# A graph layer's edge loop: its entry, its row buffers and the loop for wide groups rearranged

## The chip, the cores and the metric

The kernel runs on one core of a Trainium2 chip, in one launch. The metric is the device time of that launch in microseconds (us), as a median over runs. The engines are TensorE (PE, with its weight loads as PEld), VectorE (DVE), ScalarE (ACT), GpSimd (POOL) and SyncE (SP, which only issues transfers here).

## The reference

One graph layer with a residual and a layer norm. `x` has 6250 nodes of 128 values, `src` and `dst` are the ends of 100000 edges, sorted by `dst`.

```python
msg_in = concatenate([x[src], x[dst]], -1)                    # [100000, 256]
h = relu(msg_in @ Wm1 + bm1)                                  # hidden 256
h = relu(h @ Wm2 + bm2)                                       # 256
messages = h @ Wm3 + bm3                                      # 128
agg = segment_sum(messages, dst) / clip(count(dst), 1)        # mean over a node's edges
upd = relu(concatenate([x, agg], -1) @ Wn1 + bn1) @ Wn2 + bn2
out = layernorm(x + (x + upd))
```

All data are float32.

## The kernel before

**Algebra.** The first product is taken per node and not per edge: table A is `x @ Wm1[:128]` (float32, in DRAM, `atab`) and table B is `x @ Wm1[128:]` (split into bf16 terms, in DRAM, `btab`). An edge's hidden row is A's row of its source plus B's row of its destination. The third product is linear, so the second hidden layer is summed per destination first, in `acc`, and multiplied with `Wm3` per node afterwards.

**Stage 1 (0 to about 74 us).** Thirteen blocks of 512 nodes: load x, turn it (`turn`), A table (`a_table`), B table (`b_table`, `b_terms`), stores of both (`b_stores`, on SP's queue), and preparation of the edges' indices on DVE. `weights(i)` loads four weights. `x_part(b, ...)` is the x half of the update's first layer for one block: two matmuls of 128x512 (L355) into two PSUM banks, and an eviction each, on ACT (L358) or DVE (L360). Twelve of the blocks are done at places listed by hand: ten in `X_BEHIND` behind the table matmuls, block 9 (`X_FIRST`) in the edge loop's first step and block 10 (`X_END`, the generator `rest`) in its last. `pb3` is a small product of a weight and a bias (L451), added to `b3` as `b23`. `destinations(g, ...)` fetches the `dst` values of two groups, broadcast over the partitions, into `db` (256 KB, two transfers of 128 KB on ACT's queue). Three of these are fetched in the last three blocks of stage 1, into the three buffers of `db`.

**Stage 2, the edge loop (about 75 to 1072 us).** The edges form 196 groups of 512, handled in 98 pairs. It is a Python loop, so the program is straight-line; the order of instructions on PE and DVE is the order in which they are written (manual schedules), and the loop is a pipeline by hand over i, with p = i - 1:

- `fetch` of pair i: `rows` (2 buffers) holds for each group four gathered rows of A and the loaded rows of B side by side. Eight indirect gathers on POOL (L492) and eight loads from `btab` (L498) on SP's queue; for pair 0 the second group's four loads are on ACT's queue, behind the wait for B's stores like the other four.
- `hot`: one-hot matrices from `db` on DVE (L516, L519), one pair ahead.
- `first_layer` of pair p: 32 transposes of gathered A rows into PSUM (`ph`, L533; one buffer, so the previous pair's evictions must be done), 16 bf16 matmuls that add B's rows through the one-hots (L540), and four evictions with relu into `h1` on ACT (L546).
- For p = 0, X_FIRST's `x_part` follows (one eviction on ACT, one on DVE).
- `part_of(summed(p - 2))`: the sum over edges of a destination window (L565), copied on ACT (L573).
- `second_layer` of pair p - 1: L555 on PE, L557 (bias and relu by a maximum) on DVE, into `h2s`.
- `turned(p - 3)` and `add_up`: transposes (L584) and DVE's additions into `acc` at places read from registers (L594). `load_bases` fills those registers.
- `clear(n)`: DVE memsets of parts of `acc` (L638), before `first_layer` of pair 0 and at the end of steps 1 and 2.
- In the last step (p - 2 = 97) the two halves of X_END stand before and behind L565.

**Wide groups.** Where a group's destinations span more nodes than one window takes, a dynamic loop (L702, `tc.For_i(0, groups)`) adds the further windows. `groups` is 0 for these inputs, so its body is not run, but each engine passes the loop's entry and exit.

**Stage 3, the nodes (about 1073 to 1144 us).** Per block: `products` (L773: `Wm3` on `acc`; L775 on DVE; POOL's L778 multiplies with the reciprocal of the counts), `hidden` (L787, L788), `second` (L813, L815), and the norm (`moments`, `scaled`, store). The first two blocks take their reciprocals on DVE from `acc` (L767, L768). For the others the counts go from `acc` to `rcol` (SP, L754), reciprocals of those are stored to `rtab` (L760), and `rc` is loaded from there, broadcast (L770).

Of the kernel before, what the change touches and what calls it, by code (L numbers as in the profile page):

```python
# [19 lines left out]
P = 128  # L20
# [7 lines left out]
def kernel(  # L28
# [121 lines left out]
    with tc.tile_pool(name="prep", bufs=1) as prep, tc.tile_pool(  # L150
# [34 lines left out]
            nc.gpsimd.dma_start(bu1, bn1.rearrange("(c p) -> p c", p=P))  # L185

        def weights(block):
            for t in (wu1, w3, w2):
                nc.vector.tensor_copy(t[:, 0, :1], xT[:, block * 4 * P:block * 4 * P + 1])
            nc.gpsimd.dma_start(nb2[:, 0, :], bm2.rearrange("(o h) -> o h", o=1).to_broadcast([P, H]))  # L190
            nc.sync.dma_start(wu1, wn1.rearrange("(k p) h -> p k h", p=P))
            nc.sync.dma_start(w3, wm3.rearrange("(k p) h -> p k h", p=P))
            nc.sync.dma_start(w2, wm2.rearrange("(k p) h -> p k h", p=P))

        nc.vector.memset(xT[:, N:], 0.0)

# [178 lines left out]
        def destinations(g, ng, dst_row):  # L375

            db = ld.tile([P, 2, 2 * P], I32, name="db", bufs=3)
            if isinstance(g, int) and g < 6:

                nc.vector.tensor_copy(db[:, 0, :1], srcT[:, 0, :1])  # L380
            for h in range(2):
                edges = dst_row[:, ds(g * GE, ng * GE)].rearrange("o (s e) -> o s e", s=ng)
                edges = edges[:, :, h * 2 * P:(h + 1) * 2 * P]
                nc.scalar.dma_start(db[h * NQ:(h + 1) * NQ, :ng, :], edges.to_broadcast([NQ, ng, 2 * P]))
            return [db[:, k, :] for k in range(ng)]
# [20 lines left out]
        for i in range(BLOCKS):  # L406
            if i in X_LOADS:
                load_x(*X_LOADS[i], behind=i)
                if X_LOADS[i][1] == BLOCKS - 1:
                    nc.sync.dma_start(x_sb[:N - NTF * P, NTF, :], x[NTF * P:, :])  # L410
            for n, t0 in enumerate(range(4 * i, min(4 * i + 4, NT), 2)):

                if n == (i == 0) and i + 1 < BLOCKS:
                    turn(4 * i + 4)
                a_table(t0)
            b_stores()
            for _ in range(min(len(blank), 3 if i < BEHIND else 1)):
                nc.gpsimd.memset(blank.pop(0), 0.0)
            if i == BEHIND + 1:
                weights(i)  # L420
            if i == INDICES:
                starts()
            if i - INDICES in (1, 2):
                columns(i - INDICES - 1)
                partition_bases(i - INDICES - 1)
            if i == BLOCKS - 1:
                nc.scalar.copy(tilei, base[0:1].rearrange("p r w -> p (r w)"))
                nc.gpsimd.tensor_scalar(nb2, nb2, -1.0, None, op0=ALU.mult)
            if i >= BEHIND:
                b_block(i - BEHIND)  # L430
            if BLOCKS - 3 <= i:
                early.append(destinations(2 * len(early), 2, dst_row))
        assert not blank
        behind = list(X_BEHIND)
        with tc.manual_schedule(engines={ENG.DVE}):
            for n, j in enumerate(range(BLOCKS - BEHIND, BLOCKS)):
                if n < 4:
                    whole(x_part(behind.pop(0), bank_pb, (nc.scalar, (nc.scalar, nc.vector)[n % 2])))
                b_block(j)
                b_stores()  # L440
            b_terms()
            b_stores()
        stores.close()


        turns.enter_context(tc.manual_schedule(engines={ENG.DVE}))
        for n, b in enumerate(behind):
            whole(x_part(b, bank_pb, (nc.vector if n >= len(behind) - 2 else nc.scalar, nc.vector)))
        pb3 = pp.tile([P, 1], F32, name="pb3", tag="pp")
        for c in range(HC):  # L450
            nc.tensor.matmul(pb3, w3[:, c, :], b2[:, c:c + 1], start=(c == 0), stop=(c == HC - 1))  # L451
        nc.vector.tensor_add(b23, b3, pb3)

# [10 lines left out]
    with edge, tc.tile_pool(name="wk", bufs=2) as wk, tc.tile_pool(  # L464
# [19 lines left out]
        def fetch(groups, queues):  # L484


            rows = ld.tile([P, 2, (GT + 1) * H], F32, name="rows", bufs=2)
            got = []
            for i, ((idx, firsts), queue) in enumerate(zip(groups, queues)):
                ag = rows[:, i, :GT * H].rearrange("p (j h) -> p j h", j=GT)  # L490
# [4 lines left out]
                bw = rows[:, i, GT * H:].bitcast(BF16).rearrange("p (k h) -> p k h", k=2)  # L495
                for j, first in enumerate(firsts):
                    terms = btab[ds(first, WB + 1)].rearrange("n c h -> (n c) h")
                    queue.dma_start(bw[j // 2 * NQ:(j // 2 + 1) * NQ, j % 2, :], terms[:NQ])  # L498
# [25 lines left out]

        halves = [slice(h * NQ, (h + 1) * NQ) for h in range(2)]

        def first_layer(got, ohts, nts):
            ph = p1.tile([P, 2, 2, HC, 2 * P], F32, name="ph")
            for i, ((ag, bw), nt) in enumerate(zip(got, nts)):
                for c in range(HC):  # L530
                    for u in range(GT):
                        for h in range(nt // 2):
                            nc.tensor.matmul(ph[:, i, h, c, u * NQ:(u + 1) * NQ], ag[halves[h], u, c * P:(c + 1) * P],  # L533
                                             ident[halves[h], halves[h]], is_transpose=True,
                                             start=(c == 0 and u == 0), stop=False, skip_group_check=True)
            for i, ((ag, bw), nt) in enumerate(zip(got, nts)):
                for c in range(HC):
                    for k in range(2):
# [4 lines left out]
            for i in reversed(range(len(nts))):  # L543
                nh = nts[i] // 2
                for c in range(HC):
                    nc.scalar.activation(h1[:, i, c, :nh * 2 * P].rearrange("p (h e) -> p h e", h=nh),  # L546
                                         ph[:, i, :nh, c, :], AF.Relu, bias=b1[:, c:c + 1])
            return h1

        def second_layer(h1, h2, nt):  # L550
# [81 lines left out]
        def summed(p):  # L632
            s = st[p]
            return sums([(s["ohs"][i], h2s[i], s["nts"][i]) for i in range(2)])

        slots = list(range(SLOTS))

        def clear(n):  # L638
# [5 lines left out]
        for i in range(NP + 4):  # L644
# [54 lines left out]


        dpad_row = dpad.rearrange("(o e) -> o e", o=1)
        with tc.For_i(0, groups, 1) as g:  # L702
            more = nc.values_load(
                morei[0:1, ds(g, 1)], min_val=0, max_val=N // 16,
                skip_runtime_bounds_check_because="the difference of two nodes over 16")
            with tc.For_i(0, more, 1):
                for t, by in ((tilei[0:1, ds(g * GT, GT)], float(WB)), (pbase[:, ds(g, 1), :], float(WB)),
                              (dloc[:, ds(g, 1), :], -float(WB))):
                    nc.vector.tensor_scalar(t, t, by, None, op0=ALU.add)
                idx = wk.tile([P, GT], I32, name="idx")  # L710
                nc.vector.tensor_copy(idx, srcT[:, ds(g, 1), :].rearrange("p o j -> p (o j)"))
                pbc = wk.tile([P, 2], F32, name="pbc")
                nc.vector.tensor_copy(pbc, pbase[:, ds(g, 1), :].rearrange("p o k -> p (o k)"))
                dl = wk.tile([P, GT], F32, name="dl")
                nc.vector.tensor_copy(dl, dloc[:, ds(g, 1), :].rearrange("p o j -> p (o j)"))

                ti = wk.tile([1, GT], I32, name="ti")
                nc.vector.tensor_scalar_min(ti, tilei[0:1, ds(g * GT, GT)], float(N - 1))
                got = fetch([(idx, load_bases(ti, GT, ENG.SP))], [nc.sync])
                db, = destinations(g, 1, dpad_row)  # L720
                ohts, (oh,) = hot([(db, pbc, dl, GT)])
                h1 = first_layer(got, ohts, [GT])
                second_layer(h1[:, 0], h2s[0], GT)
                part = part_of(sums([(oh, h2s[0], GT)]), [GT])
                add_up(turned(part, [GT]), [load_bases(ti, GT, ENG.DVE)], [GT])


    NB = 4 * P
# [226 lines left out]
```

## Time and profile before

| | |
|---|---|
| Median of 6 runs | 1149.25 us (1147.84 to 1155.75) |
| The profiled execution | 1150.46 us |
| Its span, first to last instruction | 1148.4 us |
| Mean granted clock of TensorE in it | 0.995 |
| ACT, DVE and POOL busy in it | 378.6, 683.0 and 810.6 us |
| Start of the first L533 of pairs 0 to 5 | 75.33, 83.23, 92.08, 103.12, 113.84, 123.9 us |
| One pair from then on | 10.06 us |
| POOL's eight gathers of a pair | start every 10.05 us |
| B's last store: issued, landed | 67.85, 72.49 us |
| Pair 0: last L540 ends, its four L546 | 80.0, 80.16 to 82.58 us |
| First L773 of the node stage | 1073.39 us |

All rows below the median are of one profiled execution. A pair's start is the start of its first L533 matmul. The granted clock is the share of full speed that TensorE was given in a stretch. In an answer on waits, "A <- B: sum, times, longest" says that operations of A waited for B; a "q" behind an engine's name is its sequencer or queue. In a timeline each line has a start, the time from there to the end of the last of its instructions, the engine, the line of code and the operation, the number of instructions, and in brackets an idle time ahead of it and what ended it.

### The profile page before, as it was taken

Reading aid. Unit: us, or ns where it says so; the run is one execution under the profiler, and the core shown is the slowest. Engines: PE = TensorE matmul, PEld = TensorE weight load, DVE = VectorE, ACT = ScalarE, POOL = GpSimd, SP = SyncE. Lnnn points to the kernel's source line nnn. Section 1 sums busy time; section 2 is a strip of 40 time slices with the busy share of each in tenths; the row PEclk is TensorE's granted clock in tenths of the full one; section 3 lists DMA queues with packets and bytes.
Section 4 is the critical chain, followed back from the end, with each engine's and each line's share of the span. In section 5 each row is a group of like instructions: output and inputs, shape, how many; then the busy total and the mean of one; then the engine's idle time right before and its main releaser. Section 6 shows DMA issues by size and latency. Waiting matters only on the chain. (4 is left out here: it accounts for less than half of the span.)

```text
span 1148.4 us, 32176 instructions
## 1 busy us (share of the span) xinstructions
PE 1133.0 (99%) x11222; PEld 913.9 (80%) x11223; DVE 683.0 (59%) x2073; ACT 378.6 (33%) x768; POOL 810.6 (71%) x871
## 2 busy tenths in 40 slices
PE   9989999999999999999999999999999999999997
PEld 8757888888888888888888888888888888888566
DVE  5775556655555565555555555555555555555687
ACT  6752333322233332223333223333322333322165
POOL 8867777777777777777777777777777777773222
PEclk9999999999999999999999999999999999999899
DMA  8966666566666656666665656556555555552343
GB/s 283 366 227 183 170 174 172 157 177 178 169 171 176 175 153 178 178 170 170 176 166 155 168 162 161 162 154 156 158 158 161 162 160 155 155 157 63 102 126 103
DMA packets 167752, 193.67 MB, mean 169 GB/s; under 512 B 31074, under 2 KB 133428, under 8 KB 167572
## 3 DMA queue, kind: packets, MB, share of 16 engines
q0 software_dynamic: 38160, 103.75, 33.7%
q1 hardware_dynamic: 100640, 61.84, 18.4%
q10 hardware_dynamic: 28788, 26.01, 7.7%
q8 instruction: 89, 1.46, 0.5%
q14 instruction: 75, 0.61, 0.2%
HBM read 168.97 MB, written 22.88 MB: 167 GB/s over the span
## 5 line engine op out<-in xcount | busy, mean ns | idle before, releaser
L492 POOL DMA_INDIRECT rows<-atab,srcT x784 | 747.4, 953 | 244.7 <-issue 185.2
L555 PE MATMUL bank<-w,h 128*128 128x256 f32 x3128 | 701.3, 382 | 0.7 <-DVE acc L594 0.6
L555 PEld LDWEIGHTS bank<-w,h 128*128 128x128 f32 x3128 | 586.5, 190 | 116.5 <-PE bank L565 40.3
L557 DVE TENSOR_TENSOR h<-bank,nb 128x512 f32<-128x512 f32 x391 | 270.9, 693 | 349.6 <-PE bank L555 329.8
L546 ACT ACTIVATE h<-ph,b 128x512 f32<-128x512 f32 x392 | 236.7, 686 | 694.0 <-PE ph L540 665.6
L594 DVE TENSOR_TENSOR acc<-acc,bank 128x63 f32 x782 | 172.7, 221 | 69.1 <-DVE h L557 34.9
L533 PE MATMUL ph<-ident,rows 64*128 64x64 f32 x3128 | 114.2, 223 | 1.3 <-DMA rows<-atab,srcT 0.7
L533 PEld LDWEIGHTS ph<-ident,rows 64*128 64x128 f32 x3128 | 105.5, 139 | 2.9 <-ACT x_sb L358 1.0
L565 PE MATMUL bank<-h,oh 128*32 128x257 f32 x1564 | 105.5, 386 | 0.2 <-ACT x_sb L358 0.2
L516 DVE TENSOR_SCALAR oht<-db,pbase 128x128 bf16<-128x128 int32 x392 | 95.2, 294 | 0.4
L584 PEld LDWEIGHTS bank<-ident,part 64*128 64x128 f32 x1173 | 43.1, 136 | 32.9 <-issue 32.2
L573 ACT COPY part<-bank 128x257 f32<-128x257 f32 x196 | 65.3, 401 | 7.1 <-PE bank L565 7.1
L778 POOL TENSOR_TENSOR agg<-total,rc 128x512 f32<-128x512 f32 (+2 forms) x15 | 16.0, 1070 | 72.2 <-DVE total L775 37.3
L565 PEld LDWEIGHTS bank<-h,oh 128*32 128x32 f32 x1564 | 40.8, 109 | 28.3 <-DVE acc L594 0.8
L540 PE MATMUL ph<-oht,rows 64*128 64x128 bf16 x1564 | 60.9, 217 | 2.4 <-DMA rows<-btab 2.4
L584 PE MATMUL bank<-ident,part 64*128 64x64 f32 x1173 | 56.5, 229 | 0.0
L519 DVE TENSOR_TENSOR oh<-iota_n,dloc 128x128 f32<-128x128 f32 x196 | 55.5, 283 | 0.0
L540 PEld LDWEIGHTS <-rows 64*128 64x128 bf16 x1564 | 49.0, 95 | 2.8 <-DMA rows<-btab 2.7
L258 PE MATMUL pbt<-w,xT 128*128 128x256 f32 x196 | 46.0, 381 | 0.9 <-DVE rest L285 0.6
L258 PEld LDWEIGHTS pbt<-w,xT 128*128 128x128 f32 x196 | 36.0, 190 | 7.4 <-DVE rest L285 1.3
L773 PE MATMUL pmt<-acc,w 128*128 128x512 f32 (+2 forms) x60 | 26.1, 573 | 2.6 <-DVEq L702 2.6
L815 PEld LDWEIGHTS pot<-wu,u 128*128 128x128 f32 x192 | 23.6, 192 | 4.8 <-issue 4.3
(134 smaller groups left out, 419.4 us busy)
## 6 DMA issues: line engine op xcount, KB each, us to landing
rows<-btab SPq DMA_DIRECT2D x778, 32.0 KB
db<-in_dst_dram ACTq DMA_DIRECT2D x194, 128.0 KB
rows<-atab,srcT POOLq DMA_INDIRECT x784
btab<-acc SPq DMA_DIRECT2D x24, 384.0 KB
atab<-at SPq DMA_DIRECT2D x24, 256.0 KB
xd<-in_x_dram SPq DMA_DIRECT2D x12, 256.0 KB
x2tab<-xd SPq DMA_DIRECT2D x12, 256.0 KB
x_sb<-in_x_dram SPq DMA_DIRECT2D x5, 512.0 KB
```

Source lines behind the costliest of these rows:

```text
L258: nc.tensor.matmul(pbt[:, a, :], xT[:, (t0 + a) * P:(t0 + a + 1) * P], w1[:, k, :], start=True, stop=True)
L492: nc.gpsimd.indirect_dma_start(out=ag[:, j, :], out_offset=None, in_=atab[:, :], in_offset=bass.IndirectOffsetOnAxis(ap=idx[:, j:j + 1], a ...
L516: nc.vector.tensor_scalar(ohts[:n, i, k, :], db[:n, k * P:(k + 1) * P], pb_cols[:n, k:k + 1], None, op0=ALU.is_equal)
L533: nc.tensor.matmul(ph[:, i, h, c, u * NQ:(u + 1) * NQ], ag[halves[h], u, c * P:(c + 1) * P], ident[halves[h], halves[h]], is_transpose=Tru ...
L540: nc.tensor.matmul(ph[:, i, h, c, k * P:(k + 1) * P], bw[halves[h], k, c * P:(c + 1) * P], ohts[halves[h], i, k, :], start=False, stop=Tru ...
L546: nc.scalar.activation(h1[:, i, c, :nh * 2 * P].rearrange("p (h e) -> p h e", h=nh), ph[:, i, :nh, c, :], AF.Relu, bias=b1[:, c:c + 1])
L555: nc.tensor.matmul(ph2[:, j - j0, :], h1[:, c, j * P:(j + 1) * P], w2[:, c, :], start=(c == 0), stop=(c == HC - 1))
L557: nc.vector.tensor_tensor(h2[:, j0:j0 + 2, :H], ph2, nb2.to_broadcast([P, 2, H]), op=ALU.max)
L565: nc.tensor.matmul(pg[j * WN:(j + 1) * WN, :H + 1], oh[:, j, :], h2[:, j, :], start=True, stop=True, skip_group_check=True)
L573: nc.scalar.copy(part[:nt * WN, i], pg[:nt * WN, :H + 1])
L584: nc.tensor.matmul(pts[h][:, i, c, :], rows, ident[halves[h], halves[h]], is_transpose=True, start=True, stop=True, skip_group_check=True)
L594: nc.vector.tensor_add(window, window, pts[h][:, i, :, k:k + WB])
```

## The change

1. `w2` is no longer loaded in `weights`; its load stands on SP's queue behind B's last stores.
2. Of the three early `db` fetches only pair 0's stays in stage 1, three blocks before its end. Pair 1's is issued behind the `x_part`s of `X_BEHIND`, pair 2's in the edge loop.
3. `pb3` moves in among those `x_part`s.
4. `rows` becomes two tiles with two buffers each: `arows` for A's gathered rows and `brows` for B's.
5. `first_layer` takes a `between`: for pair 0, X_FIRST is put between the transposes and the one-hot matmuls, with both of its evictions on DVE, and the two `h1` evictions of the first group go to DVE, those of the second to ACT. `clear(3)` goes behind it.
6. `load_firsts`: the registers for the last two pairs' additions are loaded earlier, amid the last `second_layer`.
7. X_END is computed whole behind `turned` of the last pair.
8. The loop over wide groups becomes `If(groups > 0)` around a loop over all `NG` groups (a group that is not wide takes no step in it).

```diff
         def weights(block):
-            for t in (wu1, w3, w2):
+            for t in (wu1, w3):
...
-            nc.sync.dma_start(w2, wm2.rearrange("(k p) h -> p k h", p=P))
...
             db = ld.tile([P, 2, 2 * P], I32, name="db", bufs=3)
-            if isinstance(g, int) and g < 6:
+            if isinstance(g, int) and g < 2:
                 nc.vector.tensor_copy(db[:, 0, :1], srcT[:, 0, :1])
...
-            if BLOCKS - 3 <= i:
-                early.append(destinations(2 * len(early), 2, dst_row))
+            if i == BLOCKS - 3:
+                early.append(destinations(0, 2, dst_row))
...
             b_terms()
             b_stores()
+        nc.sync.dma_start(w2, wm2.rearrange("(k p) h -> p k h", p=P))
         stores.close()
...
         for n, b in enumerate(behind):
+            if n == 2:
+                pb3 = pp.tile([P, 1], F32, name="pb3", tag="pp")
+                for c in range(HC):
+                    nc.tensor.matmul(pb3, w3[:, c, :], b2[:, c:c + 1], ...)
+                nc.vector.tensor_add(b23, b3, pb3)
             whole(x_part(b, bank_pb, (nc.vector if n >= len(behind) - 2 else nc.scalar, nc.vector)))
-        pb3 = pp.tile([P, 1], F32, name="pb3", tag="pp")
-        for c in range(HC):
-            nc.tensor.matmul(pb3, w3[:, c, :], b2[:, c:c + 1], ...)
-        nc.vector.tensor_add(b23, b3, pb3)
+        early.append(destinations(2, 2, dst_row))
...
-            rows = ld.tile([P, 2, (GT + 1) * H], F32, name="rows", bufs=2)
+            arows = ld.tile([P, 2, GT * H], F32, name="arows", bufs=2)
+            brows = ld.tile([P, 2, 2, H], BF16, name="brows", bufs=2)
...
-        def first_layer(got, ohts, nts):
+        def first_layer(got, ohts, nts, between=None):
...
+            if between is not None:
+                whole(between)
             for i, ((ag, bw), nt) in enumerate(zip(got, nts)):
...
-                    nc.scalar.activation(h1[:, i, c, ...], ph[:, i, :nh, c, :], AF.Relu, bias=b1[:, c:c + 1])
+                    to = h1[:, i, c, :nh * 2 * P].rearrange("p (h e) -> p h e", h=nh)
+                    if between is not None and i == 0:
+                        nc.vector.tensor_scalar(to, ph[:, i, :nh, c, :], b1[:, c:c + 1], 0.0, op0=ALU.add, op1=ALU.max)
+                    else:
+                        nc.scalar.activation(to, ph[:, i, :nh, c, :], AF.Relu, bias=b1[:, c:c + 1])
...
+        def load_firsts(p):
+            st[p]["firsts"] = [load_bases(tilei[0:1, g * GT:(g + 1) * GT], NTS[g], ENG.DVE) for g in (2 * p, 2 * p + 1)]
...
-                firsts = [load_bases(tilei[0:1, g * GT:(g + 1) * GT], NTS[g], ENG.DVE) for g in (2 * k, 2 * k + 1)]
+                if k < NP - 2:
+                    load_firsts(k)
+                firsts = st[k]["firsts"]
                 pt = turned(st[k]["part"], st[k]["nts"])
+                if k == NP - 1:
+                    whole(rest)
                 add_up(pt, firsts, st.pop(k)["nts"])
...
+            if p < NP:
+                s = st[p]
+                between = x_part(X_FIRST, bank, (nc.vector, nc.vector)) if p == 0 else None
+                s["h1"] = first_layer(s.pop("got"), s.pop("ohts"), s["nts"], between)
             if p == 0:
                 clear(3)
-            if p < NP:
-                s = st[p]
-                s["h1"] = first_layer(s.pop("got"), s.pop("ohts"), s["nts"])
-            if p == 0:
-                whole(x_part(X_FIRST, bank, (nc.scalar, nc.vector)))
-            if p - 2 == NP - 1:
-                next(rest)
...
-            if p - 2 == NP - 1:
-                next(rest)
...
                 for j, nt in enumerate(s["nts"]):
+                    if p == NP and j == 1:
+                        load_firsts(NP - 2)
+                        load_firsts(NP - 1)
                     second_layer(s["h1"][:, j], h2s[j], nt)
...
-        with tc.For_i(0, groups, 1) as g:
-            more = nc.values_load(...)
-            with tc.For_i(0, more, 1):
+        with tc.If(groups > 0):
+            with tc.For_i(0, NG, 1) as g:
+                more = nc.values_load(...)
+                with tc.For_i(0, more, 1):
...
```

More of the change, by code (lines that the diff above doesn't have):

```diff
@@ L447 @@
         for n, b in enumerate(behind):
+            if n == 2:
+                pb3 = pp.tile([P, 1], F32, name="pb3", tag="pp")
+                for c in range(HC):
+                    nc.tensor.matmul(pb3, w3[:, c, :], b2[:, c:c + 1], start=(c == 0), stop=(c == HC - 1))
+                nc.vector.tensor_add(b23, b3, pb3)
             whole(x_part(b, bank_pb, (nc.vector if n >= len(behind) - 2 else nc.scalar, nc.vector)))
-        pb3 = pp.tile([P, 1], F32, name="pb3", tag="pp")
-        for c in range(HC):
-            nc.tensor.matmul(pb3, w3[:, c, :], b2[:, c:c + 1], start=(c == 0), stop=(c == HC - 1))
-        nc.vector.tensor_add(b23, b3, pb3)
+        early.append(destinations(2, 2, dst_row))
     late = ctx.enter_context(tc.tile_pool(name="late", bufs=1))
@@ L484, in fetch @@
         def fetch(groups, queues):
-            rows = ld.tile([P, 2, (GT + 1) * H], F32, name="rows", bufs=2)
+            arows = ld.tile([P, 2, GT * H], F32, name="arows", bufs=2)
+            brows = ld.tile([P, 2, 2, H], BF16, name="brows", bufs=2)
             got = []
             for i, ((idx, firsts), queue) in enumerate(zip(groups, queues)):
-                ag = rows[:, i, :GT * H].rearrange("p (j h) -> p j h", j=GT)
+                ag = arows[:, i].rearrange("p (j h) -> p j h", j=GT)
                 for j in range(GT):
@@ L494, in fetch @@
                         in_offset=bass.IndirectOffsetOnAxis(ap=idx[:, j:j + 1], axis=0))
-                bw = rows[:, i, GT * H:].bitcast(BF16).rearrange("p (k h) -> p k h", k=2)
+                bw = brows[:, i]
                 for j, first in enumerate(firsts):
@@ L545, in first_layer @@
                 for c in range(HC):
-                    nc.scalar.activation(h1[:, i, c, :nh * 2 * P].rearrange("p (h e) -> p h e", h=nh),
-                                         ph[:, i, :nh, c, :], AF.Relu, bias=b1[:, c:c + 1])
+                    to = h1[:, i, c, :nh * 2 * P].rearrange("p (h e) -> p h e", h=nh)
+                    if between is not None and i == 0:
+                        nc.vector.tensor_scalar(to, ph[:, i, :nh, c, :], b1[:, c:c + 1], 0.0,
+                                                op0=ALU.add, op1=ALU.max)
+                    else:
+                        nc.scalar.activation(to, ph[:, i, :nh, c, :], AF.Relu, bias=b1[:, c:c + 1])
             return h1
@@ L701 @@
         dpad_row = dpad.rearrange("(o e) -> o e", o=1)
[L702 to L705, printed above, removed]
-            with tc.For_i(0, more, 1):
[L707 to L725, printed above, removed]
@@ new lines @@
+        with tc.If(groups > 0):
+            with tc.For_i(0, NG, 1) as g:
+                more = nc.values_load(
+                    morei[0:1, ds(g, 1)], min_val=0, max_val=N // 16,
+                    skip_runtime_bounds_check_because="the difference of two nodes over 16")
+                with tc.For_i(0, more, 1):
+                    for t, by in ((tilei[0:1, ds(g * GT, GT)], float(WB)), (pbase[:, ds(g, 1), :], float(WB)),
+                                  (dloc[:, ds(g, 1), :], -float(WB))):
+                        nc.vector.tensor_scalar(t, t, by, None, op0=ALU.add)
+                    idx = wk.tile([P, GT], I32, name="idx")
+                    nc.vector.tensor_copy(idx, srcT[:, ds(g, 1), :].rearrange("p o j -> p (o j)"))
+                    pbc = wk.tile([P, 2], F32, name="pbc")
+                    nc.vector.tensor_copy(pbc, pbase[:, ds(g, 1), :].rearrange("p o k -> p (o k)"))
+                    dl = wk.tile([P, GT], F32, name="dl")
+                    nc.vector.tensor_copy(dl, dloc[:, ds(g, 1), :].rearrange("p o j -> p (o j)"))
+                    ti = wk.tile([1, GT], I32, name="ti")
+                    nc.vector.tensor_scalar_min(ti, tilei[0:1, ds(g * GT, GT)], float(N - 1))
+                    got = fetch([(idx, load_bases(ti, GT, ENG.SP))], [nc.sync])
+                    db, = destinations(g, 1, dpad_row)
+                    ohts, (oh,) = hot([(db, pbc, dl, GT)])
+                    h1 = first_layer(got, ohts, [GT])
+                    second_layer(h1[:, 0], h2s[0], GT)
+                    part = part_of(sums([(oh, h2s[0], GT)]), [GT])
+                    add_up(turned(part, [GT]), [load_bases(ti, GT, ENG.DVE)], [GT])
```

## The prediction

> **What bounds the kernel now.** I read the page first, then the waits, then the windows and the timeline around the two places where TensorE (PE) stands still. The page says that PE is busy throughout:
>
> ```profile
> PE 1133.0 (99%) x11222; PEld 913.9 (80%) x11223; DVE 683.0 (59%) x2073; ACT 378.6 (33%) x768; POOL 810.6 (71%) x871
> ```
>
> The timeline in mid-run shows one pair of edge groups every 10.06 us (the first L584 matmul of a pair at 505.77, of the next at 515.83), PE without a gap; POOL's eight gathers of a pair take some 10.05. The pairs from the fifth on (some 950 us) contain nothing that this diff takes from PE, so what can be won lies in the hand-over to the edge loop and in the way out of it. PE's waits name both:
>
> ```profile
> PE pmt L773 <- DVEq L702: 2.6, 1, 2.6
> PE ph L540 <- DMA rows<-btab: 2.4, 2, 1.2
> ```
>
> First is the way out, second the hand-over; the other PE waits are at most 1.1 us each. The windows (stretch and its length, then the busy time of PE, PEld, DVE, ACT and POOL, the granted clock, the DMA share and GB/s) show that each idle stretch is paid a second time, in clock:
>
> ```profile
> 75.00:80.00 5.00, 2.31 (x49) 1.81 (x49) 4.38 (x19) 0.00 (x0) 0.27 (x1) 0.93 0.35 99
> 80.00:85.00 5.00, 5.00 (x54) 2.73 (x53) 2.09 (x7) 3.00 (x5) 3.75 (x4) 0.73 0.39 112
> ...
> 1070.00:1075.00 5.00, 2.44 (x14) 1.78 (x14) 1.73 (x8) 0.69 (x1) 0.00 (x0) 0.76 0.05 6
> 1075.00:1080.00 5.00, 5.00 (x11) 2.84 (x10) 4.91 (x7) 0.00 (x0) 0.72 (x1) 0.56 0.64 174
> ```
>
> The timeline at the hand-over, each line with its start and length:
>
> ```profile
> 72.82 27.37 SPq L498 DMA_DIRECT2D rows<-btab  x33
> ...
> 79.19 0.88 PE L540 MATMUL ph<-oht,rows 64*128 64x128 bf16 x13 [1.18 <-DMA rows<-btab]
> 80.00 3.30 PE L355 MATMUL bank<-xT,wu 128*128 128x512 f32 x4
> 80.16 2.42 ACT L546 ACTIVATE h<-ph,b 128x512 f32<-128x512 f32 x4 [9.30 <-PE ph L540]
> ...
> 83.23 1.21 PE L533 MATMUL ph<-ident,rows 64*128 64x64 f32 x32
> ...
> 93.68 0.53 PE L533 MATMUL ph<-ident,rows 64*128 64x64 f32 x10 [0.70 <-DMA rows<-atab,srcT]
> ```
>
> B's rows are loaded only once B's stores have landed (72.8). Pair 0's L540 matmuls drip in behind those loads and end at 80.0. X_FIRST's matmuls (L355) then run at half clock, 3.2 us for what takes 1.72 (four passes of 0.43). Under them ACT empties `ph` by 82.6, which pair 1's L533 needs; so X_FIRST is the cover of the evictions. The way out:
>
> ```profile
> 1069.20 1.13 PE L355 MATMUL bank<-xT,wu 128*128 128x512 f32 x2
> ...
> 1070.87 1.49 DVE L594 TENSOR_TENSOR acc<-acc,bank 128x63 f32 x6 [1.41 <-PE bank L584]
> 1073.39 8.38 PE L773 MATMUL pmt<-acc,w 128*128 128x256 f32 x16 [2.56 <-DVEq L702]
> ...
> 1084.06 5.07 POOL L778 TENSOR_TENSOR agg<-total,rc 128x512 f32<-128x512 f32 x4 [3.28 <-DMA rc<-rtab]
> ```
>
> **Hand-over: when pair 0's L540 ends.** Two of three early `db` fetches (512 KB) leave the stretch before 72 us, in which the DMA share is 0.88 to 1.04. Queue q10 carries 26.01 MB in 7.7% of the span (88 us), so they are worth up to 1.7 us of landing time for B's last store. They also held ACT's queue at 47 to 50 us, behind which PE lost 0.65 at 52. w2's 256 KB leave too, but from near 29 us, where PE waits for none of it, and come back right behind the last store, in SP's queue ahead of B's row loads: 0.7 us at the 350 KB/us of 45 to 50 us. I take the stores' end at 71.0 instead of 72.5.
>
> The built program then does something that the diff does not say. ACT's four loads for pair 0's second group now share landing semaphores with others: its first waits until w2 has landed, its second for the `db` just issued, its third for SP's second load and its fourth for SP's fourth. Before, they waited for the stores alone. SP's fourth load was issued at 75.1 and used at 79.2, four us; shifted, it lands at about 77.2. ACT's fourth is issued then and needs 2.3 (ACT's first one: issued at 72.81, landed by 75.15) to 4.0 more, while POOL's gathers for pair 2, now released by pair 0's L533, run beside it. L540 thus ends at 79.5 to 81.2, bounds 78.2 and 82.0; I take 79.9, near the faster row: no gain where one is meant.
>
> **Hand-over: what follows L540.** X_FIRST (1.72) moves ahead of L540 and hides in that wait; pb3 (0.50) moves in among the pxu matmuls, and the 0.57 that L533 waited for `b23` becomes a wait for the last pxu eviction: nothing. But the cover of the evictions is gone. They are split, ACT taking two and DVE two; in the built program DVE's wait for ACT's, and pair 1's L533 waits for DVE's second. ACT's two take 1.3 (2.42 for four), DVE's 1.45 (its x evictions take 0.75 each): L533 starts about 2.85 after L540, at 82.75 against 83.23. Gain 0.5.
>
> Then the clock. Before, two idle stretches of 1.18 between 76.6 and 79.2 were enough for half clock from about 79.3 to 82.7; the loss was mostly hidden, since the evictions ran to 82.6 anyway (0.6 lost). After, PE stands for some 4 of the 4.75 us from 78.0 to 82.75, and the half-clock stretch falls on pair 1's L533 to L555: 1.7 lost (half of 3.4), 3.4 if two stretches fall there. [...] The trace halved the clock on gaps of 1.18, so I go by the trace.
>
> Pair 2's gathers start at about 76.3 instead of 80.34 and end before they are needed: the 0.70 wait at 93.68 goes, with 0.2 around it: 0.9. The 0.63 wait at 106.35 (L555 for the first `acc` additions, behind two clearing memsets on DVE) stays. Behind ACT's evictions its queue now issues pair 2's `db`; it lands near 85, when DVE has ended its memsets, and L557 has banks to spare: nothing, 1 us at worst. Sum: -0.5 + 1.7 - 0.6 (the loss already paid) - 0.9 = -0.3; but in the old kernel the gather wait absorbed part of what came before it (gathers ended at 93.6 whatever PE did), so I drop 0.7 of it: **+0.4**, bounds -3.0 and +3.5.
>
> **Way out.** X_END's two products no longer stand between the last pairs' steps. L565 of pair 97 starts at 1066.75 instead of 1067.80, its part copies end at 1068.2, L584 at 1068.7 (was 1070.83). DVE's register loads sit ahead of its last L557; its eight additions for pair 96 end at 1069.2, the six for pair 97 (0.25 each) at 1070.75 (was 1072.36). X_END's matmuls (1.72) lie beside them, ACT's two evictions end at 1071.1. Then the exit: PE went through 13 waits on every semaphore, six of them after DVE's mark, 0.86 in all (1072.53 to 1073.39). In the new program the conditional's other arm joins code that waits only for what the next matmul needs: DVE's additions and ACT's evictions. L773 at about 1071.25: -2.1. DVE's own exit list shrinks from 13 waits to 10, so its L767 comes at 1072.6 (was 1074.56).
>
> The stage behind has 5.16 us of L773 work (eight passes of 0.215, eight of 0.43) and took 8.38: 3.2 lost to clock. With 1.0 idle instead of 2.56 that may go. But the reciprocals' round trip (rcol, rtab, rc: from SP's issue at 1073.07 to POOL's first wide product at 1084.06) moves by only 1.8, so the third block cannot start before 1083.5 (was 1086.93). PE's saving ends between 1.8 and 3.4: I take **-2.5**, and -1.0 as the poor end.
>
> **Sum.** +0.4 - 2.5 = -2.1. The profiled execution took 1150.46 (span 1148.4, 2.06 around it); it lies 1.2 above the median of 1149.25, about what one half-clock stretch more or less makes. From the median: 1147.2.
>
> **Rivals.** (A) The loads land early and clock holds: L540 at 78.2, L533 at 81.05 (-2.2), no loss (-0.6), gather wait gone (-0.2 net), exit -3.3: 1143.0. For it: the DMA rows are saturated just where traffic is taken out. Against: the new semaphore waits. 0.12.
> (B) Slower: the serial loads plus serial evictions. If the stores still end at 72.5 and gathers stretch each load to 4 us, L540 ends at 82.5, L533 starts at 85.35 (+2.1), two half-clock stretches (+3.4), less 0.6 paid and 0.9 for the gathers, and the exit gives 1.0: +3.0, 1152.3. It decides from L540 ending about 1.5 after 80.0. For it: every load row under gathers takes 3 to 4 us. 0.15.
> [...] 0.13.
>
> **How the numbers follow.** Main case 0.60, within 1145 to 1149. Outside 1142.8 to 1151.5 I leave about 0.16: 0.06 below, from (A)'s far half, and 0.10 above, from (B)'s. A difference of 0.5% (5.7 us) is about what a measurement can tell from none: faster 0.08 (most of A, 1143.5 being its edge), slower 0.03 (B with more than 1155), same 0.89.
>
> **What would show it.** Right: L355 of X_FIRST at full clock between L533 and L540; ACT's fourth row load issued just as SP's fourth lands; L540's end at 79 to 81 and PE idle for 2.5 to 3 us before pair 1's L533; granted clock still below 0.9 in 80 to 90; no wait at pair 2's L533; pairs at 10.06; L773 about 2 us after the last L355 or less. Wrong: L540 ending before 78.5; PE's idle after it under 2 us; a wait of over 2 us ahead of L773; a pair period other than 10.06.

## The result and the profile after

The changed kernel took 1150.76 us (median of 32 runs, 1148.25 to 1151.97), the kernel before 1149.99 (68 runs, 1146.72 to 1156.86). The ratio, which goes by fast runs alone, is 1.0003 (the two medians give 1.0007), with a 95% interval of 0.9996 to 1.0009: between 0.5 us faster and 1.0 us slower, nothing that this measurement can tell from no change. The profiled execution took 1149.77 us, its span is 1148.0 (before 1148.4).

The page of the changed kernel, and its view of TensorE's waits (sum, times, longest):

```profile
PE 1131.6 (99%) x11222; PEld 913.1 (80%) x11223; DVE 684.1 (60%) x2073; ACT 378.0 (33%) x765; POOL 811.5 (71%) x871
```

```profile
PE ph L536 <- DVE h L553: 3.1, 1, 3.1
PE ph L545 <- DMA brows<-btab: 2.3, 3, 1.0
...
PE pmt L788 <- ACTq L716: 0.8, 1, 0.8
```

The wait for the way out has shrunk from 2.6 to 0.8 us. The wait for B's rows is as long as before, and a new wait of 3.1 us stands behind it: pair 1's transposes for the evictions of pair 0. The same in stretches of 5 us (length, busy time of PE, PEld, DVE, ACT, POOL, granted clock, DMA share, GB/s):

```profile
75.00:80.00 5.00, 3.79 (x46) 2.03 (x45) 4.76 (x18) 0.00 (x0) 2.13 (x2) 1.00 0.64 153
80.00:85.00 5.00, 0.79 (x10) 0.33 (x7) 0.88 (x2) 1.27 (x2) 3.78 (x4) 0.72 0.59 148
85.00:90.00 5.00, 4.22 (x54) 3.88 (x55) 3.75 (x10) 1.36 (x3) 3.57 (x4) 0.59 0.70 196
...
1070.00:1075.00 5.00, 3.45 (x21) 1.34 (x17) 2.98 (x14) 2.12 (x4) 0.00 (x0) 1.00 0.01 2
1075.00:1080.00 5.00, 4.92 (x16) 3.04 (x17) 4.52 (x7) 0.00 (x0) 0.72 (x1) 1.00 0.65 169
```

At the entry the loss of clock lay in 75 to 85 us before and was one half-clock stretch long (3.41 us at a granted clock of 0.5); now it lies in 80 to 90 us and is two stretches long (6.83 us). At the exit it is gone: the granted clock is 1.00 in 1070 to 1080 us, where it was 0.76 and 0.56. The timeline of the entry:

```profile
73.46 29.64 SPq L501 DMA_DIRECT2D brows<-btab  x36
74.77 5.40 ACTq L501 DMA_DIRECT2D brows<-btab  x4
...
77.15 1.98 PE L354 MATMUL bank<-xT,wu 128*128 128x512 f32 x4
77.50 1.19 POOL L495 DMA_INDIRECT arows<-atab,srcT  x1 [2.59 <-PE ph L536]
...
82.23 0.50 PE L545 MATMUL ph<-oht,brows 64*128 64x128 bf16 x5 [1.05 <-DMA brows<-btab]
82.82 0.69 ACT L556 ACTIVATE h<-ph,b 128x512 f32<-128x512 f32 x1 [11.22 <-DMA arows<-atab,srcT]
...
84.12 1.41 DVE L553 TENSOR_SCALAR h<-ph,b 128x512 f32<-128x512 f32 x2 [4.19 <-DMA arows<-atab,srcT]
85.78 1.97 PE L536 MATMUL ph<-ident,arows 64*128 64x64 f32 x32 [3.05 <-DVE h L553]
```

ACT's four row loads take 5.4 us to be issued; the one-hot matmuls end at 82.73 (before 80.07). ACT evicts two tiles, then DVE two, and TensorE stands for 3.05 us before pair 1, whose transposes then take 1.97 us instead of 1.21. And the exit:

```profile
1071.83 0.52 PE L593 MATMUL bank<-ident,part 64*128 64x64 f32 x8 [0.26 <-ACT part L582]
1072.28 1.98 PE L354 MATMUL bank<-xT,wu 128*128 128x512 f32 x4
1072.38 1.50 DVE L603 TENSOR_TENSOR acc<-acc,bank 128x63 f32 x6 [0.42 <-PE bank L593]
...
1075.08 5.43 PE L788 MATMUL pmt<-acc,w 128*128 128x256 f32 x16 [0.82 <-ACTq L716]
```

The sixteen matmuls that took 8.38 us before take 5.43. So in these two executions the change consists of a loss and a gain of about the same size. Here are both, with the starts of the pairs' first transposes and the time from pair 97's start (`put` is the tile of `hidden`'s matmuls):

| us | before | after | difference |
|---|---|---|---|
| pairs 0, 1, 2, 3 start | 75.33, 83.23, 92.08, 103.12 | 76.01, 85.78, 95.88, 106.00 | +0.68, +2.55, +3.80, +2.88 |
| pair 97 starts | 1049.51 | 1052.31 | +2.80 |
| from there to the first matmul of the node stage | 23.88 | 22.78 | -1.10 |
| to the first `put` matmul | 32.10 | 28.04 | -4.06 |
| to the end of the span | 98.87 | 95.65 | -3.22 |

The starts of the pairs also contain how long stage 1 took, and that varies: SP's first row load was issued at 72.82 before and at 73.46 after, but in two more executions with the stage 1 of the kernel before (the exit alone, and the exit with the row buffers apart, below) at 74.43 and 77.34. In the latter pair 97 starts at 1051.96, though its entry is nearly that of the kernel before. The +2.8 of one execution is therefore not yet the price of the new entry; the experiments give that.

### The profile page after: what moved, and what is told of

The parts are those of the page before. It is cut to its first block, busy times and chain, and to the rows that moved or that the text cites. A ratio compares the mean times of both kernels' runs of the same rounds, so it can differ in the third digit from the quotient of the medians.

```text
span 1148.0 us, 31479 instructions
## 1 busy us (share of the span) xinstructions
PE 1131.6 (99%) x11222; PEld 913.1 (80%) x11223; DVE 684.1 (60%) x2073; ACT 378.0 (33%) x765; POOL 811.5 (71%) x871
## 5 line engine op out<-in xcount | busy, mean ns | idle before, releaser
L495 POOL DMA_INDIRECT arows<-atab,srcT x784 | 748.4, 955 | 241.4 <-issue 211.0
L536 PE MATMUL ph<-ident,arows 64*128 64x64 f32 x3128 | 114.6, 223 | 3.9 <-DVE h L553 3.1
L536 PEld LDWEIGHTS ph<-ident,arows 64*128 64x128 f32 x3128 | 106.1, 140 | 5.3 <-issue 3.6
L545 PE MATMUL ph<-oht,brows 64*128 64x128 bf16 x1564 | 61.2, 217 | 2.3 <-DMA brows<-btab 2.3
L545 PEld LDWEIGHTS <-brows 64*128 64x128 bf16 x1564 | 49.2, 96 | 3.5 <-DMA brows<-btab 2.8
L803 PE MATMUL put<-agg,wu 128*128 128x512 f32 (+2 forms) x60 | 23.9, 517 | 0.4 <-DVE sh L865 0.4
```

What stands on the lines that cost most here:

```text
L495: nc.gpsimd.indirect_dma_start(out=ag[:, j, :], out_offset=None, in_=atab[:, :], in_offset=bass.IndirectOffsetOnAxis(ap=idx[:, j:j + 1], a ...
L545: nc.tensor.matmul(ph[:, i, h, c, k * P:(k + 1) * P], bw[halves[h], k, c * P:(c + 1) * P], ohts[halves[h], i, k, :], start=False, stop=Tru ...
```

## The experiments

The theory was that the entry costs about 3 us and the exit gives back 3 to 4. Two rivals: that either is an accident of the profiled execution; and, within the entry, that traffic and not the shared semaphores holds the row loads. Some of the runs were made on chips where a pair takes 10.06 us, as in both profiles above, others on two chips where it takes 15 to 17 us and the kernel before took 1713.76 and 1665.47 us. The totals of the latter tell nothing of an effect of 3 us, but what their traces show behind the loop is used below. The new places of w2 and `pb3` and the earlier registers were not tried each by itself.

**The way out alone**, first run. The diff to the kernel before is items 6 to 8 of the change:

```diff
+                if k == NP - 1:
+                    whole(rest)
...
-        with tc.For_i(0, groups, 1) as g:
+        with tc.If(groups > 0):
+            with tc.For_i(0, NG, 1) as g:
```

> The kernel before with only the way out changed: the conditional, X_END whole behind the last transposes, the registers of the last two pairs loaded earlier. Theory 1 (the change is two halves that cancel): pair starts as before (75.3, 83.2, 92.1, 103.1), first L773-line matmul 0.8 to 1.5 us earlier than 1073.39 and no half-clock stretch behind it, 3 to 4 us less than before in the median. Rival (the clock behind the exit comes and goes from one execution to the next, whatever the exit): 1 us less in the median, at most 1.5.

0.9972 (0.9935 to 1.0009) of 1713.76 us: inconclusive. TensorE's waits in that execution, and its page line, show why:

```profile
PE 1336.1 (79%) x11222; PEld 1050.1 (62%) x11223; DVE 659.2 (39%) x2073; ACT 381.0 (22%) x768; POOL 813.0 (48%) x871
```

```profile
PE bank L584 <- DVE h L557: 287.2, 106, 4.6
```

TensorE is idle for a fifth of the span, in every pair, and most of that is a wait for L557, which in turn waits for L555's banks (410.7 us). The next three ran on the same chip.

**The entry alone** (the changed kernel with the loop, X_END's halves and the registers as before):

> The changed kernel with the way out as before (loop over wide groups, X_END's halves around the last sums, registers loaded where they were). Theory 1: 2.5 to 3.5 us more than before; pair 1 starts near 85.8, pair 2 near 95.9, from the fifth pair on 2.8 behind the kernel before. Rival: within 1 us of before, and the late pairs of the changed kernel's trace were an accident of that execution.

1.0674 (1.0617 to 1.073) of 1713.76 us. That is neither theory's number: 112 us, lost over all pairs (a pair takes 17.1 us there, 15.6 in the run above), not at the entry.

**Pair 1's `db` early again**, first run, and **X_FIRST behind the one-hot matmuls**, first run; their diffs follow with the second runs.

> The changed kernel, but pair 1's db is fetched early again (two blocks before the end of stage 1), so that of ACT's four row loads for pair 0 only the fourth shares a landing semaphore, and only with w2. Theory 1 (the shared semaphores serialize ACT's row loads): the four are issued within 3 us of each other, pair 0's last one-hot matmul ends at 80 to 81 (82.7 in the changed kernel), pair 1 starts at 83 to 84, 1.5 to 2.5 us less than the changed kernel. Rival (w2's load and pair 2's early gathers slow the row loads by themselves): the one-hot matmuls still end after 82, under 0.7 us gained.

> The changed kernel, but X_FIRST behind pair 0's one-hot matmuls as before (one eviction on ACT, one on DVE) and all four of pair 0's evictions on ACT. Theory 1 (the cover of the evictions is what is missing): one-hot matmuls still end near 82.5, pair 1 starts at 85.0 to 85.4, but the half-clock stretch falls on X_FIRST, under the evictions; 1.5 to 2.5 us less than the changed kernel. Rival (X_FIRST costs as much behind the matmuls as the bare evictions): within 0.7 us of the changed kernel.

1.0663 (1.0601 to 1.0725) and 1.0505 (1.0434 to 1.0576): again all pairs, 17.1 and 16.9 us each. All kernels of this study with the row buffers apart that ran on these chips lost 5 to 7% there; the three with the buffers together stayed within 0.3% of before. In mid-loop the buffers are the only part of the change that plainly acts, which makes them the suspect. This is only argued: no kernel that differs in the buffers alone ran on such a chip.

**The way out alone**, again, same diff:

> The kernel before with only the way out changed, once more, where a pair takes 10.06 us in mid-loop. Theory 1 (two halves that cancel): pair starts as before, the first matmul of the node stage 0.8 to 1.5 us earlier, no half-clock stretch behind it, 3 to 4 us less than before in the median. Rival (the clock behind the exit comes and goes): about 1 us less. Should a pair take 15 us again: within 0.5% of before, as in the first run.

0.9981 (0.9969 to 0.9994): 1148.37 against 1150.47 us, 2.1 less, with an interval from 0.7 to 3.6. The exit gains in the median, and in the trace as in the changed kernel: the node stage's first matmul 22.77 after pair 97's start, the first `put` 28.04, no half-clock stretch there. In size the 2.1 lies between the theory's 3 to 4 and the rival's 1, and the interval reaches both. The end came 96.26 after pair 97's start, not 95.65: `put` had to wait once for the reciprocals' round trip.

```profile
PE put L795 <- POOL agg L785: 1.0, 1, 1.0
PE pmt L780 <- ACTq L708: 0.8, 1, 0.8
```

**Pair 1's `db` early again**, which gives the loads other landing semaphores (diff to the changed kernel):

```diff
-            if i == BLOCKS - 3:
-                early.append(destinations(0, 2, dst_row))
+            if BLOCKS - 3 <= i < BLOCKS - 1:
+                early.append(destinations(2 * len(early), 2, dst_row))
...
-        early.append(destinations(2, 2, dst_row))
```

> The changed kernel with pair 1's db fetched early again, once more. Theory 1 (shared landing semaphores serialize ACT's row loads): pair 0's one-hot matmuls end at 80 to 81, pair 1 starts at 83 to 84, 1.5 to 2.5 us less than the changed kernel, so 1 to 2.5 less than before. Rival (traffic slows the row loads by itself): one-hot matmuls end after 82, within 0.7 us of the changed kernel. Should a pair take 15 us again: 6 to 7% over before, as in the first run.

0.9994 (0.9985 to 1.0003) of before: 1149.21 us. The mechanism is as the theory has it. ACT's loads and what follows:

```profile
72.64 3.58 ACTq L500 DMA_DIRECT2D brows<-btab  x4
```

```profile
78.86 0.83 PE L544 MATMUL ph<-oht,brows 64*128 64x128 bf16 x16
...
82.74 1.21 PE L535 MATMUL ph<-ident,arows 64*128 64x64 f32 x32 [3.05 <-DVE h L552]
...
85.56 0.72 PE L544 MATMUL ph<-oht,brows 64*128 64x128 bf16 x7 [1.20 <-DMA brows<-btab]
```

The loads go out from 72.64 on (74.77 in the changed kernel), the one-hot matmuls end at 79.69 instead of 82.73, and pair 1 starts 3.04 us earlier; 0.84 of that is an earlier first row load (72.62, not 73.46). But pair 2 starts at 95.52, only 0.36 earlier: the two half-clock stretches now lie at 83.88 to 90.70, on matmuls, and pair 1 waits 1.20 us for its own rows. So the held loads cost less than they seem to: by the two ratios (1.0003 and 0.9994, each with 0.0006 to 0.0009 to either side) about 1 us. That lies between what the two theories gave, and the two intervals do not tell it from nothing.

**The way out and the row buffers apart, nothing else** (diff to the kernel before: items 4 and 6 to 8):

> The kernel before with the way out changed and the row buffers apart, nothing else. Theory 1: the entry as before up to pair 1, pair 2's gathers released by the transposes, so the 0.70 wait at pair 2 is gone: 3.5 to 4.5 us less than before, the fastest of all. Rival (the wait only moves to the additions that L555 waited for): as the exit alone. Should a pair take 15 us: if row buffers apart are what cost 6% there, this one is 5 to 7% over before; if it is the other entry parts, it is within 1%.

0.9971 (0.9959 to 0.9983): 1147.32 against 1150.47 us, the best ratio of the study and faster than both kernels. Pair 2's wait for its gathers is gone: from pair 2 to pair 3 it takes 10.11 us (11.04 before, 10.52 in the execution of the exit alone, which has the old buffers too). Whether that is really added to the exit's gain, the intervals of this run and of the exit alone cannot tell apart.

The run also prices the entry. The changed kernel differs from this one only in items 1 to 3 and 5, all of them at the entry, and its ratio is 1.0003 against 0.9971: taking the two intervals as independent, these items cost 3.7 us, 2 to 5. So the loss is in the times and not only in one execution.

**X_FIRST behind the one-hot matmuls, the rows free.** The kernel with pair 1's `db` early, and X_FIRST as cover again:

```diff
-                between = x_part(X_FIRST, bank, (nc.vector, nc.vector)) if p == 0 else None
-                s["h1"] = first_layer(s.pop("got"), s.pop("ohts"), s["nts"], between)
+                s["h1"] = first_layer(s.pop("got"), s.pop("ohts"), s["nts"])
             if p == 0:
                 clear(3)
+                whole(x_part(X_FIRST, bank, (nc.scalar, nc.vector)))
```

> As the changed kernel with pair 1's db early again (its row loads free of each other), and X_FIRST behind pair 0's one-hot matmuls as before, its evictions on ACT and DVE, all four of pair 0's evictions on ACT. Theory 1 (bare evictions leave TensorE idle for 3 us, which costs two half-clock stretches of 3.41 us on matmuls): one-hot matmuls end near 79.7, pair 1 starts at 82.5 to 83.5, one half-clock stretch instead of two, under X_FIRST; 2 to 3.5 us less than the same kernel with X_FIRST between, about 3 to 4 less than the kernel before. Rival (X_FIRST hidden in the wait for the rows is worth its 1.7 us, the idle time is not what sets the clock): within 0.7 us of the kernel with X_FIRST between, two half-clock stretches again.

0.9983 (0.9969 to 0.9996): 1147.27 us. The one-hot matmuls end at 80.32, pair 1 starts at 83.42, and there is one half-clock stretch, 79.41 to 82.82, under X_FIRST. From the first row load to pair 5's start, a count that leaves stage 1 out, it takes 49.67 us, with X_FIRST between 53.80 (and 53.33 in the changed kernel). In these profiles the cover is worth 4 us, of which 1.20 is pair 1's wait for its own rows; the edit also moves the evictions back to ACT, so it is both together. One execution is a rough scale here: the entry of the kernel before took 51.08 us by this count in its own profile and 49.61 in that of the exit alone, which has the same entry. Still, the five traces in which matmuls cover pair 0's evictions take 49.1 to 51.1 (49.10 with the exit and the row buffers apart, 49.95 in the next experiment), the two without cover 53.3 and 53.8, whether the row loads are held or free. The times alone do not settle it: by the ratios, 0.9983 against 0.9994, the cover is worth 1.3 us, and the intervals overlap. Against the changed kernel's 1.0003 free loads and cover together gain 2.3 us, 0.6 to 4.

**Both covers at the entry.** Loads as before, buffers apart, X_FIRST between, all four evictions on ACT, and X_END as the cover:

```diff
             if p == 0:
+                whole(x_part(X_END, bank, (nc.vector, nc.vector)))
                 clear(3)
```

> A version built on theory 1: w2 and the db fetches as before, row buffers apart, X_FIRST between transposes and one-hot matmuls (evictions on DVE), all of pair 0's h1 evictions on ACT, and X_END as the cover behind the one-hot matmuls (evictions on DVE) in place of the end; the way out is the conditional. Theory 1: one-hot matmuls end at 79.5 to 80.5, pair 1 starts at 82.3 to 83.3, at most one half-clock stretch, pair 2 without a wait for gathers; at the end the first matmul of the node stage comes 1 to 2 us earlier after pair 97's start than the 22.8 of the changed kernel; 4 to 6 us less than before. Rival (the node stage is held by the round trip of the reciprocals, which does not start earlier, and the entry is bound by the loads): 2.5 to 3.5 us less than before, as the exit with row buffers apart.

0.9982 (0.9973 to 0.999): 1147.63 us, 2.1 less than before, short of the theory's 4 to 6 and below the rival's 2.5 to 3.5. The entry is as expected: the matmuls end at 80.82, pair 1 starts at 83.39, and the entry has no half-clock stretch at all. The exit, though, has lost X_END:

```profile
1069.06 0.52 PE L588 MATMUL bank<-ident,part 64*128 64x64 f32 x8 [0.26 <-ACT part L577]
1069.62 1.49 DVE L598 TENSOR_TENSOR acc<-acc,bank 128x63 f32 x6 [0.42 <-PE bank L588]
...
1071.66 8.10 PE L781 MATMUL pmt<-acc,w 128*128 128x256 f32 x16 [2.08 <-DVEq L709]
```

Without X_END's 1.98 us of matmuls the node stage starts 0.66 us earlier after the last transposes, but TensorE has been idle for 2.08 us. Two half-clock stretches (1070.30 to 1077.13) follow and cost 2.7. The conditional is in both kernels, the cover in one; but this is one execution, and the table below has two exits with as long an idle time and no loss.

**The two parts of the exit, each alone**, and **the fourth of the square** (rows held, X_FIRST behind). The first two diffs are the conditional alone, and all of the exit without it.

> The kernel before with the conditional around the loop over wide groups, nothing else: X_END's halves and the registers stay where they were. Theory (the gain at the exit is the clock, and X_END's matmuls behind the last transposes are what keeps TensorE's idle time under a microsecond): the first matmul of the node stage comes about 23.3 after pair 97's start (23.9 before, 22.8 in the changed kernel), TensorE's idle time ahead of it is still about 2 us, the two half-clock stretches stay (first L788-line matmul about 31.5 after pair 97's start, 28.0 in the changed kernel), under 0.8 us less than before. Rival (the conditional makes the exit): no half-clock stretch there, 2 us less than before or more.

> The kernel before with X_END whole behind the last transposes and the registers loaded earlier, the loop over wide groups as it was. Theory (X_END's matmuls are the cover): TensorE's idle time ahead of the node stage is about 1.5 us (its walk through the 13 waits, 0.9, and the wait for ACT's last eviction), and at most one half-clock stretch follows: 1 to 2.5 us less than before. Rival (the conditional makes the exit): two half-clock stretches as before, within 0.7 us of before.

> The changed kernel with X_FIRST behind pair 0's one-hot matmuls and all four evictions on ACT, ACT's row loads still held by the shared semaphores; once more, where a pair takes 10.06 us. It is the fourth of a square: rows held or free, X_FIRST between or behind. Theory 1 (both cost, and the bare evictions by the clock): one-hot matmuls end near 82.5, pair 1 starts at 85 to 85.5, one half-clock stretch instead of two, 1 to 2 us less than the changed kernel and 1 to 2 more than with the rows free. Rival (only the held rows cost): as the changed kernel within 0.5 us.

These ran where a pair takes over 15 us: 0.9996 (0.9964 to 1.0028), 0.9993 (0.9968 to 1.0018) and 1.0577 (1.0497 to 1.0658) of 1665.47, so their totals decide nothing, and the square stays without its fourth corner in the time. The exits in the traces can be read, since behind the last pairs nothing is late. TensorE's wait ahead of the node stage with the conditional alone:

```profile
PE pmt L774 <- DVEq L702: 2.1, 1, 2.1
```

and with X_END and the registers alone:

```profile
PE pmt L779 <- DVE rc L773: 2.1, 1, 2.1
```

Together they leave 0.82. Counted from the first of the last 21 L584 transposes:

| us | to the node stage | idle ahead of it | from there to the first `put` | half-clock stretches up to it | from pair 97's start to the end |
|---|---|---|---|---|---|
| before | 7.16 | 2.56 | 8.21 | 2 | 98.87 |
| entry alone (old exit) | 7.22 | 2.62 | 6.89 | 1 | 98.09 |
| the conditional alone | 6.67 | 2.07 | 5.24 | 0 | 100.27 |
| X_END and registers alone | 7.32 | 2.10 | 5.26 | 0 | 96.59 |
| conditional without X_END | 5.39 | 2.08 | 7.94 | 2 | 97.15 |
| all of the exit (9 traces) | 6.05 (6.04 to 6.05) | 0.82 | 5.26 | 0 | 95.26 to 96.26 |

The expected 2 us of idle time with the conditional alone came, the clock loss expected with it did not. The expected 1.5 with X_END alone was 2.1, also without loss. An idle time of 2 to 2.6 us thus cost the clock in three of these rows and not in two; 0.82 did in none of the nine traces.

An early start of the node stage is not yet an early end. With the conditional alone, `put` then waits for POOL's product with the reciprocals:

```profile
PE put L789 <- POOL agg L779: 2.5, 1, 2.5
```

The reciprocals' round trip (SP's issue of `rcol` at 1591.00, POOL's first wide product at 1603.03) took 12.0 us there, 11.0 before and 9.8 in the changed kernel; a half-clock stretch followed the wait (1604.13 to 1607.54), and the end came 1.4 later than before. X_END and the registers alone brought 2.3 of the 2.6 to 3.6 that all of the exit brings. These two rows are one execution each.

## Why the prediction was right or wrong

The range (1142.8 to 1151.5) held the time and "no change that can be told" was the likeliest answer. The point, 2.1 us below the kernel before, was not reached: it was a sum of +0.4 and -2.5, and the profiled executions show +2.8 and -3.2. The main case (1145 to 1149) was missed too. That the time stayed inside the range is partly luck: the entry was 2.4 us worse than forecast, the exit 0.7 better, and the range was wide enough for the rest.

**L540's end: the step that failed.** 79.9 was predicted, with 82.0 as the late bound; it was 82.73. The mechanism was right: ACT's first load was issued 0.03 us after w2 had landed (74.77, 74.74), its second after the `db`'s landing (76.84, 76.81), its third and fourth after SP's second and fourth (77.89 and 79.69, after 77.87 and 79.67). Mis-sized was when that chain starts. The two `db` fetches taken out ahead of 72 us were to bring B's last landing forward from 72.5 to 71.0; the last two stores landed at 72.78 and 73.31, and SP's first row load was issued at 73.46. SP's fourth took 4.1 us as before, but landed at 79.67 and not at 77.2 (79.2 less the forecast's own 1.5 would have been 77.7), and so ACT's fourth was issued 2.5 late. It landed 2.5 us later, within the 2.3 to 4.0 forecast. The whole miss of 2.83 is that start and a few tenths. Whether taking the `db` fetches out brings the stores forward at all stays open: SP's first row load was issued at 72.82, 74.43, 77.34 and 74.08 in four executions with the fetches as before and at 73.46, 72.62 and 73.37 in three with one or two fewer, all where a pair takes 10.06 us. The holding itself shows apart from that: from the first row load to L540's end it took 9.27 us, in the other six traces 6.0 to 7.3. (The 350 KB/us that the prediction gives w2's load for 45 to 50 us is misread, the row says 401 GB/s; that is worth under 0.1 us.)

**The bare evictions** were put at 2.85 us and took 3.05. So pair 1's start was missed by L540's 2.83 and 0.2 more: 85.78, not 82.75.

**The clock at the entry**: 1.7 was predicted. Two stretches came (82.24 to 89.07), but the first held 2.92 us of idle time, so that the work under them lost little: pair 2 starts 10.10 us after pair 1, before 8.85, hence 1.25. The forecast was 1.7 less the 0.6 that the kernel before had already paid: about right, with two stretches where one was meant.

**The gathers**: the 0.9 came in full (pair 2 to pair 3: 10.12 against 11.04), so dropping 0.7 of it was wrong for these two executions. In that of the exit alone, where TensorE came to pair 2 0.25 us later after the start of its gathers, the old buffers cost only 0.4 (10.52), which is the way that the reason for the drop points.

**The way out**: -2.5 predicted, -3.2 measured. The first node matmul came 1.1 earlier and not 2.1. The forecast knew that it would wait for ACT's evictions of X_END, but had them end at 1071.1; counted from pair 97's start they ended 1.1 later (1074.99 in this trace), since X_END's matmuls began only at 1072.28, behind the last transposes, and that wait (0.82) ends last. The clock term of 3.2 was regained nearly in full (8.21 to 5.26).

**The rivals.** (B) had the entry right: it was to decide from L540 ending 1.5 us after 80.0, and it ended 2.7 after; its two half-clock stretches came. But it was paired with a poor exit, and the exit was as good as in (A), -3.3. A case that is wrong in one half and right in the other was not among them. The rival given 0.13, that the conditional does not make the exit cheaper, fell: TensorE's first node matmul starts 0.04 us after ACT's signal (1075.08, 1075.04). TensorE's own branch lies at 1072.02, where X_END's matmuls would hide a delay; in the version without that cover (both covers at the entry) its next instruction starts 0.54 us after the branch (1069.62, 1069.08). A delay of 2 us, which would have used up the 2.1 forecast for the first node matmul, is excluded.

## What to carry to other kernels

Where TensorE bounds a kernel, matmuls that can be put anywhere (X_FIRST, X_END) were, in these traces, worth most where they keep an idle stretch short, not where they merely hide in one: their price is their own time (1.98 us for either at full clock), the price of an uncovered stretch was the stretch (3.05 us at the changed entry, 2.56 at the old exit) and then the clock (two half-clock stretches, 6.83 us, at either place). Before moving an early fetch, look in the built program at which landing semaphores the transfers of the critical stretch come to share: held by them, pair 0's rows took 9.27 us from the first row load to L540's end, 6.0 to 7.3 in the other six traces with 10.06 us pairs. A change with two ends is to be forecast and measured end by end, since +2.8 and -3.2 look like nothing in the total; and an execution's own starting time has to be taken out before two traces are compared.

## What the runs showed of the hardware

In each of the two profiled executions the half-clock stretches start whole multiples of 3.413 us apart: at 79.27, 1072.55 and 1147.64 in the kernel before (291.0 and 313.0 of them between the first and the others), at 82.24 and 1143.78 in the changed kernel (311.0). Those that end within the execution are 3.41 us long (from 79.27) or 6.83 (from 1072.55 and from 82.24). Cut on these starts into cells of 3.413 us, with TensorE's idle time in each:

| cell from, us | TensorE idle, us | its clock | the next cell's clock |
|---|---|---|---|
| before, 75.86 | 2.37 | 1.00 | 0.50 |
| before, 79.27 | 0.00 | 0.50 | 1.00 |
| before, 1069.14 | 1.72 | 1.00 | 0.50 |
| before, 1072.55 | 0.84 | 0.50 | 0.50 |
| before, 1075.97 | 0.00 | 0.50 | 1.00 |
| before, 1140.82 | 1.41 | 1.00 | 1.00 |
| after, 78.83 | 2.31 | 1.00 | 0.50 |
| after, 82.24 | 2.92 | 0.50 | 0.50 |
| after, 85.65 | 0.13 | 0.50 | 1.00 |
| after, 1068.69 | 0.81 | 1.00 | 1.00 |
| after, 1072.11 | 0.82 | 1.00 | 1.00 |
| after, 1140.37 | 2.10 | 1.00 | 0.50 |

From 40 us on, every other cell up to the last matmuls held 0.70 us or less, at full clock, and was followed by full clock. So of the full-clock cells those with 1.72, 2.10, 2.31 and 2.37 us of idle time were followed by half clock, those with 1.41 and with 0.82 or less were not. More than that these two executions do not show.

The length of an idle stretch alone did not decide: 2.10 us were followed by no half-clock stretch with X_END alone, 2.08 by two without X_END, at a cost of 2.7. What made the difference stays open.

The kernel before took 1150 us on some chips and 1665 to 1714 on others. There its granted clock is 0.85 to 0.87 (0.99 to 1.00 on the former), and DVE comes late to what TensorE has recorded as done: in one pair of the exit-alone run the 32 L555 matmuls of four banks are recorded from 808.86 to 816.03 without a gap, and DVE's four L557 on these banks start at 811.81, at 816.28 and, the last two, from 819.16 on. What causes it stays open, and so does why the kernels with row buffers apart take 5 to 7% longer there.
